# Adding expert results up by token in DRAM instead of collecting one row per choice

## The chip, the cores and the metric

The kernel runs on one core of a Trainium2 chip. The core has a matrix engine (PE, with its weight loads shown as PEld), a vector engine (DVE), an activation engine (ACT), a general engine (POOL), which also issues the indirect DMAs, and a sequencer (SP), which issues most of the others. All DMAs share 16 DMA engines. Each engine works through its own instructions in the order in which they stand, and waits for the others by semaphores. The metric is the device time of one execution in microseconds. The matrix engine's clock is granted by a throttle; the profile shows the share.

## The reference, cut to what matters

Two layers run over 8 sequences of 256 tokens, 2048 tokens of 256 features in fp32. Each sublayer is followed by a layernorm over token plus result.

```python
x = L0_attn_x
x = _layernorm(x + _L0_attn_ref(x, ...))   # 16 heads, causal
x = _layernorm(x + _L0_ffn_ref(x, ...))    # 32 experts, 6 of them for each token
x = _layernorm(x + _L1_attn_ref(x, ...))   # a state-space mixer
x = _layernorm(x + _L1_ffn_ref(x, ...))    # 16 experts, 4 of them for each token
...
# a mixture: what is added to a token is the weighted sum of its experts, and a shared expert
act = jax.nn.silu(g) * u
routed = jnp.einsum('tef,efd,te->td', act, wd, combine)
shared = jax.nn.silu(hidden_states @ sg) * (hidden_states @ su) @ sd
return routed + shared
```

The change is about `routed`: `combine` is nonzero for 6 (or 4) experts of a token, and the sum over `e` has to bring together results that are computed in different places.

## The kernel before

Tokens are worked on in 16 tiles of 128 (`P`), in 4 groups (`NG`) of 4 tiles (`GT`). The tokens' rows stay on the chip all the time, as `xg[g][:, t, :]`.

**Stages.** The attention of the first layer runs group by group, up to about 700 us. Beside it, `route` works out, for each group, which experts a token takes, and POOL scatters a copy of the token's row to each of its experts' bucket in DRAM (`xs`, line 381). A row has 256 features and two words more: the number of the place where its result belongs (`dest`, from an iota), and its weight. Buckets are blanked at the start (`blank_buckets`, line 218): unfilled rows then carry the number `NOWHERE`. That is 105 MB of writes on SP's queue, beside the first 300 us of attention.

Then the first mixture M0 (`mixture`, `Experts.routed`). The filled rows are cut into 112 tiles of 128 rows of one expert. `step` is a software pipeline over tiles: SP loads the tile's rows (`xl`, line 653), 8 tiles ahead; PE turns them and DVE copies them out (`xT`, line 520); PE multiplies with the expert's gate and up weights (`gu`), ACT and DVE make the hidden rows (`s`, `h`), PE turns them (`hp`), DVE copies them (`hT`), PE multiplies with the down weights (`y`, line 573), ACT scales by the weight into `ys` (line 680, three buffers), and POOL scatters the 128 result rows to DRAM (line 681). The place is the number in the row: token times 6 plus the choice, so each of the 2048 x 6 results has a row of its own, and a row of `NOWHERE` is dropped by the bounds check. Since no two scatters touch the same row, `unordered` tells the scheduler that they need not wait for each other. They wait on POOL only for their `ys`.

After the last tile, `results` (line 706) has SP load, for each token tile, its 128 x 6 rows (768 KB, one DMA); it waits for all scatters. `summed` (line 775; groups 0 and 1) adds the upper half of the 6 to the lower half on DVE (128x768), has PE add the remaining 3 by matmuls with the identity, and adds that to the token; `combined` (line 765; groups 2 and 3) does all of it on DVE. `normed` is the layernorm. This is woven into the mixer of the second layer, which begins with group 0 as soon as its tokens are normed.

The second mixture M1 works in the same way: 72 tiles, its rows scattered beside the mixer, 2048 x 4 results. Its end (`after1`, line 1596) is the kernel's end: 16 gathers of 512 KB go into the large weight buffer `big`, beside the shared expert of the last group; then `finish` for each token tile: `summed`, `normed`, and the output DMA from ACT.

**What sets the order.** A scheduler orders each engine's instructions by their dependences; waits are put in by it for each reader and writer of a tile, of a buffer of a pool and of a DRAM array. `rowpool` has four buffers with the tag `r`, which `blank`, the scatters' sources `xe` and the gathered `gy` take in turn.

Of the kernel before, what the change touches and what calls it, by code (L numbers as in the profile page):

```python
# [38 lines left out]
class Moe:  # L39
# [6 lines left out]

    def __init__(self, name, n, f, top, halves, sh, ahead):
        self.name, self.n, self.f, self.top = name, n, f, top  # L50
        self.ahead = ahead
        self.tiles = (NTOK * top - n) // P + n
        self.rows = n * NTOK + (self.tiles - NTOK * top // P) * P

        self.sure = -(-((NG - 1) * GN * top - n * (P - 1)) // P)
        self.halves, self.fh = halves, f // halves


        self.usual = NTOK * top // P + n // 2

        self.cols = KC * 2 * f + halves * DM
        self.shwidth, self.shblocks = feature_blocks(sh)
        self.shcols = KC * self.shwidth + len(self.shblocks) * DM
# [20 lines left out]

NOWHERE = 1 << 20
ROW = DM + 2
M0 = Moe("m0", E0, F0, TOP0, 1, SH0, 8)
M1 = Moe("m1", E1, F1, TOP1, 2, SH1, 5)

ED = 512  # L90
HS, PD, ND = 8, 64, 64
# [8 lines left out]
def kernel(  # L100
# [84 lines left out]
    )  # L185


    disp = {}
    for m in (M0, M1):
        d = disp[m.name] = {}  # L190
        new = lambda shape, name, dt=F32: const.tile(
            shape, dt, name=f"{m.name}{name}", tag=f"{m.name}{name}"
        )
        d["xs"] = dram.tile([m.rows, ROW], F32, name=f"{m.name}xs", tag=f"{m.name}xs")

        d["ys"] = dram.tile([NTOK * m.top, DM], F32, name=f"{m.name}ys", tag=f"{m.name}ys")
# [12 lines left out]
        nc.gpsimd.iota(  # L209
            d["dest"], pattern=[[P * m.top, NTOK // P], [1, m.top]], base=0,  # L210
            channel_multiplier=m.top,
        )
        run = small.tile([P, m.n], F32, name=f"{m.name}run", tag=f"{m.name}run", bufs=2)
        nc.vector.memset(run, 0.0)
        d["run"] = run
        d["scatters"], d["results"], d["loads"], d["first"] = [], [], [], None
# [290 lines left out]
    class Experts:  # L507
# [114 lines left out]
        def routed(self, w, beside=None):  # L622
# [21 lines left out]
            def step(s, lo, hi):  # L644
# [31 lines left out]
                if lo <= i < hi:  # L676
                    y = self.down(hT.pop(i), wdn, bass.ds(experts[i], 1), f"{m.name}{i}")
                    row = xl.pop(i)
                    ys = self.sb.tile([P, DM], F32, name=f"{m.name}ys{i}", tag="ys", bufs=3)
                    nc.scalar.activation(ys, y, AF.Copy, scale=row[:, DM + 1 :])  # L680
                    ins = nc.gpsimd.indirect_dma_start(  # L681
                        out=d["ys"],
                        out_offset=bass.IndirectOffsetOnAxis(
                            ap=row[:, DM : DM + 1].bitcast(I32), axis=0
                        ),
                        in_=ys, in_offset=None, bounds_check=NTOK * m.top - 1, oob_is_err=False,
                    )
                    unordered(ins, f"{m.name}ys", d["results"])
                extra()
                if beside and s >= 4 and s % 2 == 0:  # L690
                    next(beside, None)
# [14 lines left out]
    def results(m, g, t, gy=None):  # L706

        d, i = disp[m.name], g * GT + t
        if gy is None:
            gy = rowpool.tile([P, m.top, DM], F32, name=f"{m.name}gy{g}_{t}", tag="r")  # L710
        ins = nc.sync.dma_start(
            gy,
            d["ys"][i * P * m.top : (i + 1) * P * m.top, :].rearrange(
                "(p k) d -> p k d", k=m.top
            ),
        )
        d["first"] = after_all(ins, d["first"], d["results"])
        return gy

    def root_by_steps(y, v):  # L720

# [42 lines left out]

    def combined(m, g, t, gy):

        half = m.top // 2
        x = xg[g][:, t, :]
        nc.vector.tensor_add(gy[:, :half, :], gy[:, :half, :], gy[:, half:, :])
        nc.vector.tensor_add(x, x, gy[:, 0, :])  # L770
        for k in range(1, half):
            nc.vector.tensor_add(x, x, gy[:, k, :])
        normed(g, t)

    def summed(m, g, t, gy, y=None, behind=None):

        half = m.top // 2
        x = xg[g][:, t, :]
        ins = nc.vector.tensor_add(gy[:, :half, :], gy[:, :half, :], gy[:, half:, :])  # L779
        if behind is not None:  # L780
            tc.add_manual_dep(ins.ins, behind.ins.name, NOSYNC, reason="it waits for longer")
# [7 lines left out]
        nc.vector.tensor_add(x, x, y)  # L789
        normed(g, t)  # L790

    def top_weights(scores, n_exp, top):
# [114 lines left out]
    with ExitStack() as st:  # L907
# [30 lines left out]
        nc.gpsimd.memset(blank[:, :, DM : DM + 1].bitcast(I32), NOWHERE)  # L938
        blank_buckets(M0, blank)
        blank_buckets(M1, blank)  # L940

        def project_v(g, q, xT):
            vs = []
# [652 lines left out]
    def after1(ex):  # L1596

        last = (NG - 1) * GT
        order = [0, 1, last, 2, 3, last + 1, 4, 5, 6, 7, last + 2, 8, 9, last + 3, 10, 11]

        rows = {}
        for n, i in enumerate(order):
            gy = big[:, n * TOP1 * DM : (n + 1) * TOP1 * DM]
            rows[i] = results(M1, *divmod(i, GT), gy.rearrange("p (k d) -> p k d", d=DM))

        def finish(i, y=None):
            g, t = divmod(i, GT)
            summed(M1, g, t, rows.pop(i), y)
            nc.scalar.dma_start(out_rows[i * P : (i + 1) * P, :], xg[g][:, t, :])

        steps = ex.shared(NG - 1, wsh1, lambda t, y: finish(last + t, y))
        for _ in range(len(M1.shblocks)):
            next(steps)
        for i in order:
            if i >= last:
                if i == last + 2:
                    next(steps)
                next(steps)
            else:
                finish(i)  # L1620
# [96 lines left out]
```

## Time and profile before

| | us |
|---|---|
| median of 17 runs | 1509.02 (1499.89 to 1514.05) |
| the profiled execution | 1500.77 |
| its span, first to last instruction | 1499.1 |
| PE busy | 1410.1 (94%) |
| DVE busy | 820.1 (55%) |
| ACT busy | 545.7 (36%) |
| POOL busy | 461.8 (31%) |
| result scatters on POOL, M0 | 112 of 989 ns |
| result scatters on POOL, M1 | 72 of 984 ns |

The profile is one execution; its busy times are the time that an engine had work under way. The page cuts the span into 40 slices of 37.5 us: the DMA engines are busy nine tenths in the first eight (the blanks), hardly at all up to about 560 us, then loaded with the expert weights and the mixtures' rows; the granted clock falls below full in the slices around 710, 950 and 1250 us, where PE has pauses. HBM is read for 79.77 MB and written for 154.88 MB.

### The profile page before, as it was taken

To read this page: it belongs to the slowest core of one execution; us is meant where nothing else is said; L and a number is where in the kernel's file an instruction comes from. 1 tells how busy PE (TensorE), PEld (TensorE's weight loads), DVE (VectorE), ACT (ScalarE), POOL (GpSimd) and SP (SyncE) were. 2 spreads that over 40 slices of the span, in tenths; PEclk is the share of its full clock that TensorE was granted. 3 is DMA by queue.
4 is the path that set the end of the run, shared out by engine and by line. 5 is a ranking of instruction groups with operands and counts; after the bars stand their busy time and mean duration, and the time that the engine had idled before them with its cause. 6 is when DMAs were issued, how large, how long until landed. Compare 5 with 4: busy or idle time off the path is not lost. (4 is left out here: it accounts for less than half of the span.)

```text
span 1499.1 us, 21445 instructions
## 1 busy us (share of the span) xinstructions
PE 1410.1 (94%) x6424; PEld 1006.7 (67%) x6424; DVE 820.1 (55%) x3004; ACT 545.7 (36%) x1453; POOL 461.8 (31%) x684
## 2 busy tenths in 40 slices
PE   8999999999999999997788898889999989999997
PEld 4666666676666666666667776546577767777766
DVE  3444465555544465545345554488678864544436
ACT  3333342333333333333234433255655432233323
POOL 1000003500052000621655556102006275633335
PEclk9999999999999999998899999799999989999999
DMA  9999999930010001242345443530001542333327
GB/s 361 413 413 413 413 411 400 364 73 1 7 50 30 0 1 60 106 157 90 121 123 187 130 145 116 222 118 32 1 1 58 210 142 89 107 107 96 96 90 265
DMA packets 79206, 232.97 MB, mean 155 GB/s; under 512 B 11067, under 2 KB 43610, under 8 KB 77680
## 3 DMA queue, kind: packets, MB, share of 16 engines
q1 hardware_dynamic: 60208, 187.26, 34.3%
q0 software_dynamic: 16576, 42.19, 7.9%
q10 hardware_dynamic: 2304, 2.10, 0.4%
q8 instruction: 56, 0.92, 0.2%
q14 instruction: 62, 0.51, 0.1%
HBM read 79.77 MB, written 154.88 MB: 157 GB/s over the span
## 5 line engine op out<-in xcount | busy, mean ns | idle before, releaser
L963 PE MATMUL qkp<-xT,big 128*128 128x512 f32 x512 | 241.2, 593 | 0.0
L998 ACT ACTIVATE pr<-neg,least 128x128 f32<-128x128 f32 (+1 forms) x256 | 114.3, 448 | 283.7 <-DVE least L993 276.1
L971 DVE COPY qk<-qkp 128x512 f32<-128x512 f32 x64 | 44.2, 690 | 176.8 <-PE qkp L963 176.7
L963 PEld LDWEIGHTS qkp<-xT,big 128*128 128x128 f32 x512 | 90.7, 191 | 69.4 <-issue 67.9
L681 POOL DMA_INDIRECT m0ys<-m0ys,m0xl x112 | 110.8, 989 | 84.8 <-issue 25.9
L381 POOL DMA_INDIRECT m0xs<-m0xe,m0rows x96 | 94.8, 988 | 111.5 <-DVE total L1002 33.9
L947 PE MATMUL vp<-big,xT 128*128 128x512 f32 x256 | 118.4, 601 | 4.6 <-DVE x L1034 4.6
L1029 PE MATMUL op<-big,z 128*128 128x256 f32 x512 | 120.5, 382 | 0.0
L993 DVE CUSTOM_DVE_ANT_0 neg<-sc,cmask 128x128 f32<-128x128 f32 (+1 forms) x256 | 81.3, 355 | 59.9 <-PE sc L983 58.8
L1029 PEld LDWEIGHTS op<-big,z 128*128 128x128 f32 x512 | 92.6, 190 | 15.0 <-ACT z L1051 4.2
L681 POOL DMA_INDIRECT m1ys<-m1ys,m1xl x72 | 70.8, 984 | 98.8 <-ACT m1ys L680 90.6
L260 POOL TENSOR_TENSOR rstd<-rstd,numbers 128x1 f32<-128x1 f32 x16 | 8.7, 551 | 282.7 <-DVE rstd L259 282.7
L947 PEld LDWEIGHTS vp<-big,xT 128*128 128x128 f32 x256 | 47.2, 193 | 49.7 <-issue 42.4
L1016 PE MATMUL zp<-pT,big 128*128 128x256 f32 x256 | 76.8, 381 | 0.1
L983 PE MATMUL sc<-qk,qk 128*128 128x256 f32 x256 | 76.5, 380 | 0.0
L1004 DVE TENSOR_SCALAR pr<-pr,total 128x128 f32<-128x128 f32 (+1 forms) x256 | 73.4, 336 | 3.4
L381 POOL DMA_INDIRECT m1xs<-m1xe,m1rows x64 | 63.0, 985 | 20.1 <-POOL m1xe L376 12.5
L1010 PEld LDWEIGHTS pt<-ident,pr 128*128 128x128 f32 x384 | 47.4, 142 | 32.4 <-issue 29.8
L1014 DVE COPY pT<-pt 128x384 f32<-128x384 f32 x128 | 67.0, 549 | 2.9 <-PE pt L1010 2.1
L1016 PEld LDWEIGHTS zp<-pT,big 128*128 128x128 f32 x256 | 47.7, 190 | 30.4 <-issue 12.0
L979 PEld LDWEIGHTS sc<-qk,qk 128*128 128x128 f32 x256 | 43.7, 190 | 22.4 <-issue 20.2
L953 ACT COPY big<-vp 128x512 f32<-128x512 f32 x53 | 31.0, 585 | 74.8 <-PE vp L947 74.8
(2756 smaller groups left out, 3024.5 us busy)
## 6 DMA issues: line engine op xcount, KB each, us to landing
m0xs<-blank SPq DMA_DIRECT2D x9, 7740.0 KB
m1xs<-blank SPq DMA_DIRECT2D x4, 7740.0 KB
m0xl<-m0xs SPq DMA_DIRECT2D x112, 129.0 KB
m0gy<-m0ys SPq DMA_DIRECT2D x16, 768.0 KB
m1xl<-m1xs SPq DMA_DIRECT2D x72, 129.0 KB
big<-m1ys SPq DMA_DIRECT2D x16, 512.0 KB
big<-in_w_moe SPq DMA_DIRECT2D x1, 5472.0 KB
big<-in_w_heads SPq DMA_DIRECT2D x12, 384.0 KB
```

Source lines behind the costliest of these rows:

```text
L381: ins = nc.gpsimd.indirect_dma_start(out=d["xs"], out_offset=bass.IndirectOffsetOnAxis(ap=rows[:, k, t : t + 1], axis=0), in_=xe[:, k, :], ...
L681: ins = nc.gpsimd.indirect_dma_start(out=d["ys"], out_offset=bass.IndirectOffsetOnAxis(ap=row[:, DM : DM + 1].bitcast(I32), axis=0), in_=y ...
L947: nc.tensor.matmul(ps, lhsT=xT[:, k, t * P : (t + 1) * P], rhs=w_vq[q][:, k, :], start=(k == 0), stop=(k == KC - 1),)
L963: nc.tensor.matmul(ps, lhsT=w_qk[h][:, at : at + P], rhs=xT[:, k, :], start=(k == 0), stop=(k == KC - 1),)
L983: nc.tensor.matmul(sc[:, P:], lhsT=qT[:, c0 + P : c0 + SEQ], rhs=kT[:, c0 : c0 + SEQ], start=True, stop=True,)
L993: nc.vector.tensor_tensor_reduce(out=neg[:, cols], in0=sc[:, cols], in1=cmask[:, cols], scale=-SCALE, scalar=3.0e38, op0=ALU.add, op1=ALU.min,
L998: nc.scalar.activation(pr[:, cols], neg[:, cols], AF.Exp, bias=least[:, i : i + 1], scale=-1.0, accum_out=total[:, i : i + 1],)
L1004: nc.vector.tensor_scalar_mul(pr[:, cols], pr[:, cols], total[:, i : i + 1])
L1010: nc.tensor.transpose(pt[:, i * P : (i + 1) * P], pr[:, i * P : (i + 1) * P], ident)
L1014: pace[0] = nc.vector.tensor_copy(pT, pt)
L1016: nc.tensor.matmul(zps[:, b * SEQ : (b + 1) * SEQ], lhsT=vs[2 * b][:, cols], rhs=pT[:, : 2 * P], start=True, stop=False,)
L1029: nc.tensor.matmul(ps[:, :DM], lhsT=zs[i][:, t * P : (t + 1) * P], rhs=w_o[q * QH + i], start=(i == 0), stop=(i == QH - 1),)
```

## The change

Each result row is no longer stored in a place of its own, but added in DRAM to a row that belongs to its token. M0 has three such arrays, M1 two (`sums`); tile i adds to array i modulo `sums`. So the scatter gets `compute_op=ALU.add`, `dest` holds the token's number alone, and the arrays have 2048 + 128 rows. Since additions to one array must not overlap, `unordered` is gone: each scatter waits for the landing of the one before it in the same array. The bounds check is gone too: a DVE instruction takes the smaller of the row's number and `nobody`, which is 2048 plus the partition, so that unfilled rows are added to 128 rows that nobody reads. The arrays must begin at zero: a tile of zeros is written over all five at the start, 15 DMAs on SP behind the blanks.

Gathering takes `sums` DMAs of 128 KB a token tile for M0 (3 x 16 in place of 16), and 2 DMAs of 256 KB for each pair of token tiles for M1 (16 in place of 16, of half the size). `summed` and `combined` have no pairwise addition any more.

```diff
@@ Moe, its two instances
-M0 = Moe("m0", E0, F0, TOP0, 1, SH0, 8)
-M1 = Moe("m1", E1, F1, TOP1, 2, SH1, 5)
+M0 = Moe("m0", E0, F0, TOP0, 1, SH0, 8, 3)
+M1 = Moe("m1", E1, F1, TOP1, 2, SH1, 5, 2)
@@ at the start
+    nobody = const.tile([P, 1], I32, name="nobody", tag="nobody")
+    nc.gpsimd.iota(nobody, pattern=[[0, 1]], base=NTOK, channel_multiplier=1)
...
+            d["ys"] = [
+                dram.tile([NTOK + P, DM], F32, name=f"{m.name}ys{i}", tag=f"{m.name}ys{i}")
+                for i in range(m.sums)
+            ]
...
-            d["dest"], pattern=[[P * m.top, NTOK // P], [1, m.top]], base=0,
-            channel_multiplier=m.top,
+            d["dest"],
+            pattern=[[P, NTOK // P], [0, m.top]] if m.sums
+            else [[P * m.top, NTOK // P], [1, m.top]],
+            base=0, channel_multiplier=1 if m.sums else m.top,
@@ step, the scatter of a tile's results
-                    ins = nc.gpsimd.indirect_dma_start(
-                        out=d["ys"],
-                        out_offset=bass.IndirectOffsetOnAxis(
-                            ap=row[:, DM : DM + 1].bitcast(I32), axis=0
-                        ),
-                        in_=ys, in_offset=None, bounds_check=NTOK * m.top - 1, oob_is_err=False,
-                    )
-                    unordered(ins, f"{m.name}ys", d["results"])
+                    if m.sums:
+                        to = self.sb.tile([P, 1], I32, name=f"{m.name}to{i}", tag="to", bufs=4)
+                        nc.vector.tensor_tensor(
+                            to, row[:, DM : DM + 1].bitcast(I32), nobody, ALU.min
+                        )
+                        d["results"].append(nc.gpsimd.indirect_dma_start(
+                            out=d["ys"][i % m.sums],
+                            out_offset=bass.IndirectOffsetOnAxis(ap=to, axis=0),
+                            in_=ys, in_offset=None, compute_op=ALU.add,
+                        ))
...
@@ results
+    def sums_of(m, gy, g, t, n):
+
+        at = (g * GT + t) * P
+        for i, ys in enumerate(disp[m.name]["ys"]):
+            nc.sync.dma_start(
+                gy[:, :, i, :], ys[at : at + n * P, :].rearrange("(t p) d -> p t d", p=P)
+            )
@@ combined and summed
-        half = m.top // 2
+        half = m.sums or m.top // 2
...
-        nc.vector.tensor_add(gy[:, :half, :], gy[:, :half, :], gy[:, half:, :])
+        if not m.sums:
+            nc.vector.tensor_add(gy[:, :half, :], gy[:, :half, :], gy[:, half:, :])
@@ behind the blanks
+        zeros = rowpool.tile([P, 6, DM], F32, name="zeros", tag="r")
+        nc.gpsimd.memset(zeros, 0.0)
+        for m in (M0, M1):
+            for ys in disp[m.name]["ys"] if m.sums else ():
+                n = (NTOK + P) // P
+                for at in range(0, n, 6):
+                    c = min(6, n - at)
+                    nc.sync.dma_start(
+                        ys[at * P : (at + c) * P, :].rearrange("(p c) d -> p c d", p=P),
+                        zeros[:, :c, :],
+                    )
@@ after1, the kernel's end
-        for n, i in enumerate(order):
-            gy = big[:, n * TOP1 * DM : (n + 1) * TOP1 * DM]
-            rows[i] = results(M1, *divmod(i, GT), gy.rearrange("p (k d) -> p k d", d=DM))
+        pairs = [0, last, 2, 4, 6, last + 2, 8, 10]
+        for n, i in enumerate(pairs):
+            gy = big[:, n * 2 * M1.sums * DM : (n + 1) * 2 * M1.sums * DM].rearrange(
+                "p (t k d) -> p t k d", t=2, d=DM
+            )
+            sums_of(M1, gy, *divmod(i, GT), 2)
+            rows[i], rows[i + 1] = gy[:, 0], gy[:, 1]
```

More of the change, by code (lines that the diff above doesn't have):

```diff
@@ L39, with __init__ @@
 class Moe:
-    def __init__(self, name, n, f, top, halves, sh, ahead):
+    def __init__(self, name, n, f, top, halves, sh, ahead, sums):
         self.name, self.n, self.f, self.top = name, n, f, top
         self.ahead = ahead
+        self.sums = sums
         self.tiles = (NTOK * top - n) // P + n
@@ L194 @@
         d["xs"] = dram.tile([m.rows, ROW], F32, name=f"{m.name}xs", tag=f"{m.name}xs")
-        d["ys"] = dram.tile([NTOK * m.top, DM], F32, name=f"{m.name}ys", tag=f"{m.name}ys")
+        if m.sums:
[3 more added lines that the diff above has]
+            ]
+        else:
+            d["ys"] = dram.tile(
+                [NTOK * m.top, DM], F32, name=f"{m.name}ys", tag=f"{m.name}ys"
+            )
         d["base"] = new([P, m.n], "base")
@@ L680, in step @@
                     nc.scalar.activation(ys, y, AF.Copy, scale=row[:, DM + 1 :])
-                    ins = nc.gpsimd.indirect_dma_start(
-                        out=d["ys"],
-                        out_offset=bass.IndirectOffsetOnAxis(
-                            ap=row[:, DM : DM + 1].bitcast(I32), axis=0
-                        ),
-                        in_=ys, in_offset=None, bounds_check=NTOK * m.top - 1, oob_is_err=False,
-                    )
-                    unordered(ins, f"{m.name}ys", d["results"])
+                    if m.sums:
+                        to = self.sb.tile([P, 1], I32, name=f"{m.name}to{i}", tag="to", bufs=4)
[7 more added lines that the diff above has]
+                        ))
+                    else:
+                        ins = nc.gpsimd.indirect_dma_start(
+                            out=d["ys"],
+                            out_offset=bass.IndirectOffsetOnAxis(
+                                ap=row[:, DM : DM + 1].bitcast(I32), axis=0
+                            ),
+                            in_=ys, in_offset=None, bounds_check=NTOK * m.top - 1, oob_is_err=False,
+                        )
+                        unordered(ins, f"{m.name}ys", d["results"])
                 extra()
@@ L709, in results @@
         if gy is None:
-            gy = rowpool.tile([P, m.top, DM], F32, name=f"{m.name}gy{g}_{t}", tag="r")
+            gy = rowpool.tile([P, m.sums or m.top, DM], F32, name=f"{m.name}gy{g}_{t}", tag="r")
+        if m.sums:
+            sums_of(m, gy.unsqueeze(1), g, t, 1)
+            return gy
         ins = nc.sync.dma_start(
@@ L775, in summed @@
     def summed(m, g, t, gy, y=None, behind=None):
-        half = m.top // 2
+        half = m.sums or m.top // 2
         x = xg[g][:, t, :]
-        ins = nc.vector.tensor_add(gy[:, :half, :], gy[:, :half, :], gy[:, half:, :])
-        if behind is not None:
-            tc.add_manual_dep(ins.ins, behind.ins.name, NOSYNC, reason="it waits for longer")
+        if not m.sums:
+            ins = nc.vector.tensor_add(gy[:, :half, :], gy[:, :half, :], gy[:, half:, :])
+            if behind is not None:
+                tc.add_manual_dep(ins.ins, behind.ins.name, NOSYNC, reason="it waits for longer")
         fresh = y is None
@@ L788, in summed @@
             )
-        nc.vector.tensor_add(x, x, y)
+        ins = nc.vector.tensor_add(x, x, y)
+        if m.sums and behind is not None:
+            tc.add_manual_dep(ins.ins, behind.ins.name, NOSYNC, reason="it waits for longer")
         normed(g, t)
@@ L940 @@
         blank_buckets(M1, blank)
+        zeros = rowpool.tile([P, 6, DM], F32, name="zeros", tag="r")
[8 more added lines that the diff above has]
+                        zeros[:, :c, :],
+                    )
         def project_v(g, q, xT):
@@ L1601, in after1 @@
         rows = {}
-        for n, i in enumerate(order):
-            gy = big[:, n * TOP1 * DM : (n + 1) * TOP1 * DM]
-            rows[i] = results(M1, *divmod(i, GT), gy.rearrange("p (k d) -> p k d", d=DM))
+        pairs = [0, last, 2, 4, 6, last + 2, 8, 10]
+        for n, i in enumerate(pairs):
+            gy = big[:, n * 2 * M1.sums * DM : (n + 1) * 2 * M1.sums * DM].rearrange(
+                "p (t k d) -> p t k d", t=2, d=DM
+            )
+            sums_of(M1, gy, *divmod(i, GT), 2)
+            rows[i], rows[i + 1] = gy[:, 0], gy[:, 1]
         def finish(i, y=None):
```

## The prediction

> **What bounds the kernel now.** I read the table by stage first, because the page's share of 94% for PE is a mean over unlike stages.
>
> ```profile
> core 0: us, PE busy (x) PEld busy (x) DVE busy (x) ACT busy (x) POOL busy (x), PEclk, DMA share, GB/s
> 790.00:936.00 146.00, 127.36 (x754) 107.75 (x753) 72.20 (x257) 58.07 (x170) 85.88 (x87) 1.00 0.45 140
> 960.00:1000.00 40.00, 34.53 (x98) 19.83 (x98) 26.00 (x65) 19.42 (x33) 2.77 (x8) 0.79 0.32 115
> 1000.00:1200.00 200.00, 191.32 (x984) 135.59 (x984) 161.13 (x566) 111.64 (x246) 48.18 (x90) 0.98 0.17 67
> 1300.00:1470.00 170.00, 166.28 (x788) 124.58 (x788) 73.61 (x208) 51.46 (x129) 66.43 (x71) 0.98 0.35 113
> 1470.00:1499.00 29.00, 19.39 (x87) 15.44 (x85) 19.31 (x69) 9.54 (x17) 16.34 (x43) 0.94 0.63 227
> ```
>
> 790 to 936 us is the first mixture's steady part: PE is busy 127 of 146 us, so some other engine's lateness is in the pace. 1300 to 1470 is the second mixture: PE 98%, nothing to gain or to lose until something else gets slower than PE. The two places where sums are collected (960 to 1000, 1470 to 1499) have PE gaps. Then POOL's own timeline, which shows the pace of the result scatters (columns: start, duration, and in brackets the idle time before and what ended it):
>
> ```profile
> 837.03 0.98 POOL L681 DMA_INDIRECT m0ys<-m0ys,m0xl  x1 [0.30 <-issue]
> 838.32 0.98 POOL L681 DMA_INDIRECT m0ys<-m0ys,m0xl  x1 [0.30 <-issue]
> 840.78 0.98 POOL L681 DMA_INDIRECT m0ys<-m0ys,m0xl  x1 [1.48 <-ACT m058s L533]
> 1360.24 0.98 POOL L681 DMA_INDIRECT m1ys<-m1ys,m1xl  x1 [1.51 <-ACT m1ys L680]
> 1362.72 0.98 POOL L681 DMA_INDIRECT m1ys<-m1ys,m1xl  x1 [1.51 <-ACT m1ys L680]
> 1456.34 0.98 POOL L681 DMA_INDIRECT m1ys<-m1ys,m1xl  x1 [1.82 <-ACT m1ys L680]
> ```
>
> In the first mixture POOL goes as fast as it can (0.98 + 0.30 = 1.29 us), then rests: tile 24 issues at 790.00 and tile 111 at 936.16, so 146.16 / 87 = 1.68 us a tile. In the second it is even, 2.49 us a tile, with 1.51 us to spare. Last, what a scatter takes to land, read where somebody waits for it:
>
> ```profile
> 1452.17 0.47 ACT L680 ACTIVATE m1ys<-m170y,m1xl 128x256 f32<-128x256 f32 x1 [0.57 <-DMA m1ys<-m1ys,m1xl]
> 1455.59 0.47 ACT L680 ACTIVATE m1ys<-m171y,m1xl 128x256 f32<-128x256 f32 x1 [2.95 <-DMA m1ys<-m1ys,m1xl]
> 1458.98 20.79 SPq L711 DMA_DIRECT2D big<-m1ys  x16
> 1462.23 0.69 DVE L779 TENSOR_TENSOR big<-big 128x512 f32<-128x512 f32 x1 [1.04 <-DMA big<-m1ys]
> ```
>
> The last scatter issues at 1456.34 and SP, which waits for it, starts the gathers at 1458.98: 2.64 us from issue to landing. The first gather needs 1462.23 - 1458.98 = 3.25 us until DVE has its rows. The two ACT rows show the end of the mixture waiting for scatters three tiles back (three `ys` buffers).
>
> **Fill.** 5 arrays of 2176 rows of 1 KB are 11.1 MB more on SP's queue behind the blank rows, which go at 413 GB/s by the page's slices: 27 us. No scatter of the first mixture's rows waits for them, since they are issued last. But the `zeros` tile holds one of four row buffers, and POOL's copy into that buffer waits for the fill. These are the rows where the like wait ends now, and POOL's next work:
>
> ```profile
> 306.42 0.23 POOL L369 COPY m0xe<-m0dest 128x6 int32<-128x6 int32 x1 [7.76 <-DMA m0xs<-m0xe,m0rows]
> 340.99 1.09 POOL L260 TENSOR_TENSOR rstd<-rstd,numbers 128x1 f32<-128x1 f32 x2 [34.34 <-DVE rstd L259]
> ```
>
> 306.4 + 27 = 333.4, and POOL is wanted at 341.0 for group 1's layernorm: hidden, with 7.6 us of cover; without it each us late delays that layernorm. The memset (the blank's, of the same size, is 1.43 us) lies in POOL's idle first 170 us. Zero.
>
> **Index.** 184 `min` operations of 128x1 on DVE at 0.15 us (DVE's 128x1 TENSOR_TENSOR). DVE is half idle in both mixtures (72 of 146, 74 of 170 us). In the changed program's order the `min` of tile k stands before the xT copy of tile k+4 and waits for the landing of scatter k-4 (four `to` buffers); behind it are that copy, hT and h, so a late landing reaches PE two steps on. In exchange a row load no longer waits for the scatter that read its index: that wait wasn't binding. Zero by itself; its wait is part of the loop below.
>
> **The new waits.** A scatter now waits on POOL for the one three tiles back (first mixture) or two back (second), because it adds to the same array. What stands behind it on POOL is the next scatter, and early in the mixture row scatters. The first of these is no news: ACT already waits for the scatter three back, through its buffer. So both are one loop: landing, ACT 0.47 us, hand to POOL 0.28, a hop of 0.1, next landing. Three tiles cost at least L + 0.85 us, and 3 x 1.68 = 5.04, so the pace holds while L, the time from issue to landing, is under 4.2 us. In the second mixture the loop is L + about 0.15 for two tiles against 4.98: L may be 4.8.
>
> No row shows an adding scatter. From below: as a plain one, 2.64. From above: the plain one and a whole gather (a read of DRAM) in series, 2.64 + 3.25 = 5.9. I take the middle, 4.3, since 128 rows must be read as well as written but the read needn't be a whole 512 KB gather. POOL's 0.98 us per scatter is bounded likewise: 0.98, or twice that if the reads' descriptors cost as much as the writes'; nearest is 0.98 with some more, which the 1.68 covers up to 1.4.
> At L = 4.3 the loop gives (4.3 + 0.85) / 3 = 1.72 us: 0.04 x 87 = 3 us. Besides, PE's work is 127.4 / 87 = 1.46 us a tile, and the other 0.22 comes from releases that arrive late. Once the loop has no slack, such a delay is partly on top: between 0 and 0.22 x 87 = 19 us; I take half, 9. Together +12. The second mixture: (4.3 + 0.15) / 2 = 2.2 < 2.49, zero. At the end of each mixture PE waits for a buffer, that is for a landing (the 2.95 us above): 1.6 us later each, +3.
>
> The Trainium skill (DMA: Bandwidth & Descriptors, Anatomy of one DMA) fits a POOL-issued DMA as 2.0 us plus its bytes at 436 GB/s; for 128 KB that is 2.3 us, where the row has 2.64. Doubling the bytes there, an estimate, adds only 0.3 us, and by it no loop binds and the sum is the gains alone. The same page (Rules for kernel authors) says that an accumulate reads its destination and writes it later, so that the earlier DMA's semaphore must be waited for: the waits can't be dropped. No run here shows that.
>
> **Gains.** The reads halve (768 to 384 KB, 512 to 256 KB a token tile) and the first pairwise add goes.
>
> ```profile
> L769 DVE TENSOR_TENSOR m0gy<-m0gy 128x768 f32<-128x768 f32 x8 | 7.6, 950 | 3.6 <-DMA m0gy<-m0ys 3.6
> L779 DVE TENSOR_TENSOR m0gy<-m0gy 128x768 f32<-128x768 f32 x8 | 7.6, 955 | 1.7 <-DMA m0gy<-m0ys 1.7
> L779 DVE TENSOR_TENSOR big<-big 128x512 f32<-128x512 f32 x16 | 10.8, 677 | 1.9 <-DMA big<-m1ys 1.9
> ```
>
> That is 26 us of DVE, but PE's work stays as it was (the matmul count by `summed` is 3 and 2 as before), so only PE's gaps can close: 1.3 us before the first sum at 949.2 (its gather is hidden beside the shared expert, 935 to 948, and so is the time that SP needs for three DMAs in place of one); 2.3 us of PE at 976 to 978 where DVE is full; 0.4 in 1000 to 1200, at 96%; and in the tail the PE gaps of 0.2, 0.5 and 1.3 us between 1481 and 1486, plus 1 us of POOL's queue of norms. Sum -7.
>
> **Sum.** +12 + 3 - 7 = +8 us on the profiled execution's own 1500.77 us (span 1499.1): 1509. That execution is 8.25 us under the median 1509.02; on the median's scale 1517.
>
> **Rivals.** Nothing binds (L under 4.2, POOL under 1.4): the gains less a little at the ends, -7 + 1: 1503, faster. For it: the plain landing has 1.5 us of slack, and 16 DMA engines are busy only 0.45. Against: the first mixture already issues in bursts. It decides at L = 4.2.
> Cancelled: gains and losses within 3 us of each other, 1509.
> Adding is dear: L = 5.9 gives 6.75 / 3 = 2.25 us, +0.57 x 87 = 50, and the second mixture 3.0 against 2.49 over 58 tiles (1305 to 1450 us), +31; ends +6, gains -7: 1589. Or POOL at 2 x 0.98 + 0.30 = 2.27 a tile: +51, 1556. Against it: the packets' share of the engines is small.
> That PE's gaps are not closed at all, since other waits stand behind them, takes the -7 away: 1524, within the forecast.
>
> **How the numbers follow.** Forecast 0.37 (own range 1512 to 1530), nothing binds 0.35, cancelled 0.12, dear 0.16. About 0.2%, 3 us, is what a measurement can tell from no change: faster 0.35, same 0.12, slower 0.53. The range runs from a little under 1503 to where about half of the dear case is cut off: 1500 to 1562.
>
> **What would show it.** The scatters' spacing between 790 and 936 (1.68 now; I say about 1.8), and the second mixture's 2.49 unchanged; POOL idle before a scatter put down to the scatter itself rather than to ACT; PE's restart after each mixture; the copy after the fill near 333. If the fill ends after 341, if DMA_INDIRECT takes over 1.4 us, or if the second mixture's pace moves, I'm wrong.

## The result, and the profile after

The changed kernel takes 1546.65 us (median, 1544.31 to 1551.93), the kernel before 1508.64 beside it: ratio 1.0261, 95% interval 1.0244 to 1.0278. That is 38 us more, where 8 were forecast. The profiled execution takes 1543.65 us, span 1541.9, which is 42.8 more than the first profile of before (1499.1).

The kernel before itself has two times: 1507 to 1509 beside the result and e1 to e8, 1471 to 1473 beside e9 to e18, at a granted clock of 0.972 and 0.978; one chip appears on both sides. Its traces tell the two apart (e13). Every ratio below is with runs of the kernel before taken beside it. Where times from the two sides are compared with each other, the time of before is given.

Where the 42.8 us lie, read from the POOL, DVE and PE timelines of the two profiles:

| | before | after | later by |
|---|---|---|---|
| result scatter of tile 24, first mixture | 790.0 | 799.4 | 9.4 |
| last result scatter of the first mixture (tile 111) | 936.2 | 971.2 | 35.0 |
| last matmul of the mixer's output (`out`) ends | 1232.3 | 1254.9 | 22.6 |
| DVE starts the last group's routing (`mx`) | 1244.1 | 1278.9 | 34.9 |
| first result scatter of the second mixture | 1281.3 | 1316.6 | 35.3 |
| last one | 1456.3 | 1499.2 | 42.8 |
| end of the span | 1499.1 | 1541.9 | 42.8 |

So there are three losses (first mixture 35, start of the second 12, inside the second 8) and a gain of 12 between the mixtures. The two mixtures' steady parts by the table by stage, with the columns that the prediction showed:

```profile
core 0: us, PE busy (x) PEld busy (x) DVE busy (x) ACT busy (x) POOL busy (x), PEclk, DMA share, GB/s
799.00:970.00 171.00, 135.56 (x756) 110.16 (x755) 74.06 (x338) 62.13 (x170) 134.56 (x88) 0.98 0.78 126
1340.00:1512.00 172.00, 165.82 (x777) 123.28 (x776) 70.07 (x253) 50.96 (x127) 101.24 (x70) 0.98 0.64 108
```

In the first, 87 tiles take 171.7 us (1.97 each) where they took 146.2; POOL is as busy as PE, and the DMA engines' share is 0.78 where it was 0.45, though fewer bytes move a second. DVE is no busier. The page's costliest groups after, where each line ends with the busy time, the mean of one, and the idle time before them with what ended most of it:

```profile
L703 POOL DMA_INDIRECT m0ys<-m0ys,m0to x112 | 174.6, 1559 | 55.8 <-issue 12.8
L703 POOL DMA_INDIRECT m1ys<-m1ys,m1to x72 | 112.0, 1555 | 65.6 <-ACT m1ys L697 10.3
L700 DVE TENSOR_TENSOR m0to<-m0xl,nobody 128x1 int32<-128x1 int32 x112 | 18.0, 160 | 124.9 <-DMA m0ys<-m0ys,m0to 118.7
L700 DVE TENSOR_TENSOR m1to<-m1xl,nobody 128x1 int32<-128x1 int32 x72 | 11.5, 160 | 109.1 <-DMA m1ys<-m1ys,m1to 92.5
```

Two things are new. An adding scatter holds POOL for 1.56 us where the plain one took 0.99. And DVE stands idle 125 + 109 us in front of the 184 index minima, nine tenths of it (118.7 + 92.5) waiting for a scatter's landing: 118.7 / 112 = 1.06 us for each of the first mixture's. The minima themselves are 0.16 us. How much of this idle time reaches the kernel's time, the experiments show. POOL's timeline, which showed bursts and rests before, has scatters as close as they go, and some rests put down to a landing:

```profile
855.39 1.55 POOL L703 DMA_INDIRECT m0ys<-m0ys,m0to  x1 [0.44 <-DMA m0ys<-m0ys,m0to]
857.25 1.56 POOL L703 DMA_INDIRECT m0ys<-m0ys,m0to  x1 [0.30 <-DMA m0ys<-m0ys,m0to]
859.11 1.55 POOL L703 DMA_INDIRECT m0ys<-m0ys,m0to  x1 [0.30 <-ACT m059s L550]
```

DVE's timeline in the first mixture's steady part (start, duration, in brackets the idle time before and what ended it):

```profile
857.14 0.16 DVE L700 TENSOR_TENSOR m0to<-m0xl,nobody 128x1 int32<-128x1 int32 x1 [0.91 <-DMA m0ys<-m0ys,m0to]
857.22 0.42 DVE L537 COPY m059xT<-m059xp 128x256 f32<-128x256 f32 x1
857.57 0.28 DVE L563 COPY m056hT<-m056hp 96x128 f32<-96x128 f32 x1
857.76 0.24 DVE L552 TENSOR_TENSOR m058h<-m058s,m058gu 128x96 f32<-128x96 f32 x1
859.58 0.16 DVE L700 TENSOR_TENSOR m0to<-m0xl,nobody 128x1 int32<-128x1 int32 x1 [1.58 <-DMA m0ys<-m0ys,m0to]
```

The copy xT, the copy hT and the product h run without a pause once the minimum is through: they were ready and stood behind it. Between the mixer and the second mixture, the same view shows the 12 us. First the last group's routing in the kernel before, then the changed kernel:

```profile
1244.06 0.22 DVE L832 TENSOR_REDUCE mx<-m1lg 128x4 f32<-128x64 f32 x1 [3.02 <-issue]
```

```profile
1263.37 0.42 DVE L580 TENSOR_TENSOR m1s_1h<-m1s_1s,m1s_1gu 128x256 f32<-128x256 f32 x1 [1.03 <-ACT m1s_1s L579]
1276.73 0.16 DVE L700 TENSOR_TENSOR m1to<-m1xl,nobody 128x1 int32<-128x1 int32 x1 [12.94 <-DMA m1xl<-m1xs]
...
1278.87 0.16 DVE L700 TENSOR_TENSOR m1to<-m1xl,nobody 128x1 int32<-128x1 int32 x1 [0.33 <-DMA m1xl<-m1xs]
1278.94 0.22 DVE L875 TENSOR_REDUCE mx<-m1lg 128x4 f32<-128x64 f32 x1
```

The logits `m1lg` were ready at 1266.8 (the end of their matmuls), but four minima of the second mixture's first tiles stand ahead of `mx` in DVE's order, and they wait for row loads. SP issues these at 1274.59, 3 us after POOL has issued the last scatter of the rows that they read:

```profile
1264.92 1.85 PE L325 MATMUL m1lg<-w_gate,m1xT 128*128 128x16 f32 x16
1271.61 0.98 POOL L398 DMA_INDIRECT m1xs<-m1xe,m1rows  x1 [0.28 <-POOL m1xe L393]
1274.59 5.52 SPq L670 DMA_DIRECT2D m1xl<-m1xs  x10
```

Nobody waited that early before, because the first user of a row was PE; there `mx` starts 0.04 us behind the end of the logits.

At the kernel's end the last scatter issues at 1499.16 and SP's gathers, which wait for its landing, follow 2.94 us later (2.64 before):

```profile
1499.16 1.55 POOL L703 DMA_INDIRECT m1ys<-m1ys,m1to  x1 [0.70 <-DMA m1ys<-m1ys,m1to]
1502.10 11.16 SPq L755 DMA_DIRECT2D big<-m1ys  x16
```

### The profile page after: what moved, and what is told of

It reads as the page before. It is cut to its first block, busy times and chain, and to the rows that moved or that the text cites. A ratio compares the mean times of both kernels' runs of the same rounds, so it can differ in the third digit from the quotient of the medians.

```text
span 1541.9 us, 21653 instructions
## 1 busy us (share of the span) xinstructions
PE 1421.7 (92%) x6424; PEld 1010.0 (65%) x6424; DVE 804.7 (52%) x3156; ACT 550.7 (36%) x1453; POOL 562.8 (37%) x686
## 3 DMA queue, kind: packets, MB, share of 16 engines
q0 software_dynamic: 34240, 45.32, 17.1%
## 4 chain that ended last, share of the span: by engine, by line
PE 68%; DMA 12%; issue 8%; POOL 6%; DVE 4%; ACT 1%; POOLq 0%; DVEq 0%; ACTq 0%; SPq 0%
PE qkp L1017 14%; DMA m0ys<-m0ys,m0to 7%; PE vp L1001 7%; PE op L1083 6%; PE zp L1070 4%; PE sc L1037 4%; DMA m1ys<-m1ys,m1to 3%; PE pt L1064 3%; POOL m1xs L398 3%; PE sc L1033 2%; PE cv L1268 2%; PE zp L1074 2%; PE gtp L1443 2%; DMA m1xs<-m1xe,m1rows 1%; PE sg L1381 1%
## 5 line engine op out<-in xcount | busy, mean ns | idle before, releaser
L703 POOL DMA_INDIRECT m0ys<-m0ys,m0to x112 | 174.6, 1559 | 55.8 <-issue 12.8
L703 POOL DMA_INDIRECT m1ys<-m1ys,m1to x72 | 112.0, 1555 | 65.6 <-ACT m1ys L697 10.3
L700 DVE TENSOR_TENSOR m0to<-m0xl,nobody 128x1 int32<-128x1 int32 x112 | 18.0, 160 | 124.9 <-DMA m0ys<-m0ys,m0to 118.7
L700 DVE TENSOR_TENSOR m1to<-m1xl,nobody 128x1 int32<-128x1 int32 x72 | 11.5, 160 | 109.1 <-DMA m1ys<-m1ys,m1to 92.5
```

Source lines behind the costliest of these rows:

```text
L703: d["results"].append(nc.gpsimd.indirect_dma_start(out=d["ys"][i % m.sums], out_offset=bass.IndirectOffsetOnAxis(ap=to, axis=0), in_=ys, i ...
```

## The experiments

**e1: the minima late.** The scheduler is told to put a tile's minimum behind the newest `hT` copy on DVE.

```diff
-            nc.vector.tensor_copy(hT, ps)
+            self.turn = nc.vector.tensor_copy(hT, ps)
...
-                        nc.vector.tensor_tensor(
+                        ins = nc.vector.tensor_tensor(
                             to, row[:, DM : DM + 1].bitcast(I32), nobody, ALU.min
                         )
+                        tc.add_manual_dep(ins.ins, self.turn.ins.name, NOSYNC, reason="late")
```

> The changed kernel with one order added: the index minimum of a tile stands on DVE behind the newest hT copy, so that it can't run ahead of the routing of the last group. Nothing is left out. In the changed kernel DVE stood 12.9 us before the first four minima of the second mixture (1263.8 to 1276.7 us), whose rows weren't there yet, and the routing behind them was late by that. Theory A (these early minima cost the whole stall): the mixture starts 12 us earlier, 1546.65 - 12 = about 1535. Theory B (the stall only covers another wait of the routing): no more than 3 us less, 1544 or more. For the first mixture: if its 1.97 us a tile is POOL's 1.55 + 0.30 with DVE's waits for landings (the minima's) on top, its 87 tiles come down to 1.86 x 87 = 162 us from 172, 10 us more, and the time is 1525; if the landings themselves bind, the pace stays at 1.97.

1514.91 us beside 1507.01: 1.0051 (1.0032 to 1.0070). 32 of the 38 us are gone with one line of order and nothing else changed. Theory A holds, and more came than the 1525 to 1535 expected. The groups and DVE's timeline of e1:

```profile
L700 DVE TENSOR_TENSOR m0to<-m0xl,nobody 128x1 int32<-128x1 int32 x112 | 17.3, 154 | 7.7 <-DMA m0ys<-m0ys,m0to 7.5 <-issue 0.2
L700 DVE TENSOR_TENSOR m1to<-m1xl,nobody 128x1 int32<-128x1 int32 x72 | 11.1, 155 | 3.3 <-DMA m1ys<-m1ys,m1to 2.5 <-DVE m1to L700 0.8
```

```profile
1254.28 0.23 DVE L876 TENSOR_REDUCE mx<-m1lg 128x4 f32<-128x64 f32 x1 [3.02 <-PE m1lg L325]
```

The idle time before the minima is 11 us in place of 234, and the routing starts on the logits. The first mixture's pace comes to 1.911 us a tile, not to POOL's 1.86.

**e6: late in the first mixture alone** (e1's dependency under `if m is M0`).

> The changed kernel with late minima in the first mixture alone; those of the second stay early. Nothing is left out. It splits the 32 us between the two mixtures. If the second mixture's share is the routing stall (12 us) and its pace (2.54 in place of 2.45, 5 us): 1515 + 17 = about 1530, between 1526 and 1534. If the first mixture's pace is most of it: under 1522.

1535.53 beside 1508.02. So the early minima cost 1546.65 - 1535.53 = 11 us in the first mixture and 1535.53 - 1514.91 = 21 in the second, over the 17 expected (1535.53 is just outside the 1526 to 1534). `mx` is 13.5 us behind the logits there, and tiles 8 to 66 of the second mixture take 2.57 us each, in e1 2.45.

**e12: eight index buffers in place of four** (`bufs=8`; `xl` has one buffer less).

> The changed kernel with eight index buffers in place of four (one row buffer less for want of room). Nothing is left out. A reader's first remedy for a wait on four buffers. In the program's order the minimum of tile k then stands as much earlier as its buffer comes free earlier, so it still waits for the newest landing. Theory (the place in the order is the cost): no help, the pace of the first mixture stays above 1.95 and eight minima stand before the second mixture's routing in place of four: 1544 or more. Rival (four buffers are too few): the pace falls to 1.91 and the time by 10 us or more, to 1536 or less.

1562.36 us (two runs), against 1546.65 (before at 1508) and 1552.84 (e14, before at 1472) with four: no help. In DVE's order the minimum of tile k now stands ahead of the xT copy of tile k, where with four buffers it stood ahead of that of tile k+4: the longer queue is used to put the minima four tiles earlier. Five minima stand ahead of `mx`, not the eight expected; `mx` is 14.2 us behind the logits, the first mixture's pace 2.11 (2.10 in e14).

**e11: no minima.** `to` is the row's own number, and the adding scatter gets the bounds check back.

```diff
-                        nc.vector.tensor_tensor(
-                            to, row[:, DM : DM + 1].bitcast(I32), nobody, ALU.min
-                        )
+                        to = row[:, DM : DM + 1].bitcast(I32)
...
                             in_=ys, in_offset=None, compute_op=ALU.add,
+                            bounds_check=NTOK - 1, oob_is_err=False,
```

> The changed kernel without the index minima: the adding scatter keeps the bounds check that the kernel before had, and unfilled rows are dropped by it. Nothing is left out. No DVE instruction waits for a landing any more, and none stands ahead of the routing. Theory (the minima's place in DVE's order is the cost, not their 0.16 us of work): the same as e1 with its late minima, 1511 to 1518. Rival (the scatter's waits, which now come through the row buffers, or the check in the scatter cost): over 1520.

1516.67 us, within 2 us of late minima (e1's 1514.91, though before is at 1471 here and at 1507 there): the place is the cost, not the work. POOL's 1.56 us a scatter stays.

**e4 and e17: the new waits alone**, in the kernel before.

```diff
                     unordered(ins, f"{m.name}ys", d["results"])
+                    n = 3 if m is M0 else 2
+                    if len(d["results"]) > n:
+                        tc.add_manual_dep(
+                            ins.ins, d["results"][-1 - n].ins.name, SYNC, reason="one at a time"
+                        )
```

> The kernel before with the new waits alone: each result scatter waits for the one three back (first mixture) or two back (second), plain scatters of 0.98 us into rows of their own. Theory POOL: plain landings are early enough (2.64 us, under 4.2), the pace stays at 1.68, the time within 4 us of before: 1505 to 1513. Theory landing: the pace goes up by 0.1 us or more, +9 us or more: 1518 and above.

> e4 once more (the kernel before with the waits between scatters alone), which was the same as before at 1508. Where the kernel before runs at 1473: 1471 to 1477 if a landing takes under 3.6 us when scatters are 1.47 us apart; 1485 or more if the waits bring the pace up to 1.6 or more.

0.9999 (0.9978 to 1.0020) beside 1507.01, 0.9998 (0.9985 to 1.0010) beside 1472.45. With plain landings the waits are free at either pace. What they cost with the longer landing of an adding scatter, these two can't tell; e8 and e10 bear on that.

**e3 and e16: POOL's time alone**, in the kernel before: one more small POOL instruction behind each result scatter, 0.58 us.

```diff
...
+                    more = nc.gpsimd.tensor_tensor(spare, ones[:, :1], root[:, :1], ALU.pow)
+                    tc.add_manual_dep(more.ins, ins.ins.name, NOSYNC, reason="behind it")
...
```

> The kernel before with one 128x1 power on POOL (0.55 us) after each result scatter, and nothing else of the change: POOL then needs 0.98 + 0.55 and the gaps, about 1.8 to 1.95 us a tile, like the adding scatter's 1.86, with no new waits, no minima and no more DMA work. Theory POOL: the first mixture's pace goes from 1.68 to 1.9 - 2.0, +19 to +28 us, and the first tiles, where row scatters alternate with results, add some 5: 1530 to 1542. Theory landing: POOL's issue has slack, and the time stays under 1514.

> e3 once more (the kernel before with 0.57 us more of POOL per scatter). POOL needs 1.81 us a tile whatever the releases do, so against 1.47 it should now cost (1.81 - 1.47) x 87 = 30 us in the first mixture where it cost 4.8 against 1.68: 1500 to 1512 beside 1473. Rival (POOL's price is hidden as it was): 1480 or less.

e3: 1511.80 beside 1507.01, 1.0039 (1.0020 to 1.0058): 5 us, far under the 23 to 35 that the theory asked for, though the pace went to 1.825. e16: 1514.45 beside 1472.45, 1.0280 (1.0260 to 1.0300): 42 us, more than the 30. The kernel with the burden takes nearly the same time in both; it is the kernel without it that differs.

**e13: the kernel before, with a trace from where it takes 1473.**

> The kernel before, unchanged, with a profile of its own. In the last call its runs took 1471.5 us beside 1508 in all earlier ones, at the same granted clock (0.978), and e9 to e12 were compared with those. Reading A (something outside the kernel's own order, in that call alone): 1505 to 1510 again, and the profile's stages lie within some 6 us of the first one's: first mixture at 1.68 us a tile, second at 2.49. Reading B (the kernel before has a second speed of its own): it comes up in some of these runs as well, near 1471, and if the profiled run is one of them its stages show where 36 us are saved, the second mixture's 2.49 us a tile first.

1473.93 beside 1473.04: reading B, but the second mixture is not where the time is saved. Its POOL timeline, in place of the bursts and rests that the prediction showed:

```profile
839.73 0.98 POOL L681 DMA_INDIRECT m0ys<-m0ys,m0xl  x1 [0.43 <-ACT m0ys L680]
841.14 0.98 POOL L681 DMA_INDIRECT m0ys<-m0ys,m0xl  x1 [0.43 <-ACT m0ys L680]
842.56 0.98 POOL L681 DMA_INDIRECT m0ys<-m0ys,m0xl  x1 [0.43 <-ACT m0ys L680]
843.97 0.98 POOL L681 DMA_INDIRECT m0ys<-m0ys,m0xl  x1 [0.43 <-ACT m0ys L680]
```

It is even, 1.41 us apart here and 1.471 from tile 24 to 111, where the first profile had 1.680: (1.680 - 1.471) x 87 = 18 us, and tile 24 is 11 us earlier: the 29 us between the two spans. The second mixture is 2.494 in both. What differs is how soon ACT follows PE. These are the `gu` matmuls of a tile and ACT's silu of them, first in the first profile (0.65 us from the one's end to the other's start), then in e13 (0.04):

```profile
842.15 0.81 PE L528 MATMUL m060gu<-big,m060xT 128*128 x4
843.61 0.25 ACT L533 ACTIVATE m060s<-m060gu 128x96 f32<-128x96 f32 x1 [1.01 <-PE m056y L573]
```

```profile
839.00 0.81 PE L528 MATMUL m070gu<-big,m070xT 128*128 x4
839.85 0.25 ACT L533 ACTIVATE m070s<-m070gu 128x96 f32<-128x96 f32 x1 [0.40 <-PE m070gu L528]
```

In the first profile the silu starts over 0.6 us after the end of the matmuls in 31 of the first mixture's last 86 tiles (in 21 of them ACT stood idle just before), here in 2. The other traces with plain scatters in the first mixture and nothing added on POOL fall apart in the same way: e2, e4, e5 and e7, beside a before of 1507 or 1508, have 16 to 31 such tiles, e15, e17 and e18, beside 1472 or 1473, have 2 to 5. Each engine has its instructions of the first mixture in the same order in both traces of before, so it isn't another schedule. What makes the releases late was not found.

**e14: the changed kernel where before takes 1472.**

> The changed kernel, unchanged, beside a kernel before that now runs at 1473 us because its first mixture goes at PE's own 1.47 us a tile (e13) where it went at 1.68 with late releases. Theory (the changed kernel's first mixture is set by POOL's 1.86 and DVE's waits, whatever the releases do): 1540 to 1550 as before, +70 us over the kernel before. Rival (its 1.97 held late releases too): 1510 to 1525. If the kernel before comes at 1508 here, +38 as measured.

1552.84 beside 1472.45: 1.0544 (1.0527 to 1.0562), 80 us. It is 6 us slower than in the result, a little over the 1540 to 1550 expected, where the kernel before is 36 us faster. There was nothing for it to gain: the silu is over 0.6 us late in 1 of its 86 tiles here, and in 1 of 86 in its first profile as well.

**e2, e5 and e15: no addition.** The changed kernel with `compute_op=ALU.add` left out (e2), and the same with late minima (e5, e15).

> The changed kernel with plain scatters in place of adding ones: what is left out is the addition in DRAM, so each array holds the last result written to a token and the output is not the reference's. Waits between scatters, index minima, fill and halved gathers stay. Theory POOL (the adding scatter costs POOL 1.55 us in place of 0.98, and 1.86 us a tile sets the first mixture's pace): the scatter goes back to 0.98 us, tile 24 to 111 takes 1.68 to 1.75 us a tile in place of 1.97, and the time falls by 20 to 25 us in the first mixture and some 5 among the first tiles of both: 1515 to 1522. Theory landing (the wait for the scatter before in the same array sets it): the pace stays between 1.9 and 1.97 and the time above 1538.

> e1 with plain scatters: late minima, waits between scatters, fill and halved gathers, and no addition in DRAM (left out, so the output is not the reference's). What remains is waits, which cost nothing by e4, and the gains. Theory: the gains are there (half the gather, no pairwise sums, -4 to -7 us): 1500 to 1503 against before's 1507, and e1 minus this, some 12 to 15 us, is what the adding itself costs. Rival: the gains never reach PE, and it is the same as before, 1506 to 1509; then adding costs 6 to 9 us. With the early minima of e2 gone, the routing stall of 12 us before the second mixture must be gone too.

> e5 once more (plain scatters, late minima, halved gathers; the addition is left out), which was 6.7 us under the kernel before at 1508. Where the kernel before runs at 1473: if waits, minima and gathers cost or gain the same there, 1464 to 1470; if the waits for landings bind at 1.47 us a tile (three tiles are 4.4 us, less 0.85 leaves 3.6 us for a landing), its first mixture stays at 1.6 to 1.7 and it takes 1485 to 1502.

e2: 1514.88 beside 1507.01, 1.0043 (1.0017 to 1.0069). Pace 1.726, and the routing stall is still there (`mx` 14.4 us behind the logits). e5: 1501.28 beside 1508.02, 0.9960 (0.9940 to 0.9980): a gain of 6.7. e15: 1460.19 beside 1472.45, 0.9918 (0.9900 to 0.9937): a gain of 12.3, more than expected. Waits, late minima, fill and gathers together are better than free. The rest of the change's price is the addition: 1514.91 - 1501.28 = 14 us by e1 and e5, 1516.67 - 1460.19 = 56 by e11 and e15 (before at 1471 and 1472; e11 has no minima at all, e15 late ones).

The two causes don't simply add up. Late minima alone take off 32 us (e1), and so does leaving out the addition alone (e2); both together take off 45 (e5). So the early minima cost 1514.88 - 1501.28 = 14 us with plain scatters and 32 with adding ones.

**e8 and e10: freer landings in the first mixture.** e1 with `M0 = Moe("m0", E0, F0, TOP0, 1, SH0, 6, 6)`, five `ys` and eight `to` buffers (e8); e9 with four arrays, four `ys` buffers and `ahead` 7 (e10).

> e1 with six arrays, five ys buffers and eight index buffers in the first mixture (row loads six tiles ahead for want of room): no scatter waits for a landing soon after it. Nothing is left out, but the gathers have six rows again and three more arrays are filled. Theory POOL: the pace of tiles 24 to 111 goes from 1.91 to POOL's own 1.86 and not under it. Theory landing: it falls towards 1.68. The fill of 8 arrays, 17.8 MB at 413 GB/s, takes 43 us from 306, to 349: the layernorm of group 1 on POOL (at 341 now) should be some 8 us late, and the whole kernel that much later if nothing makes up for it.

> e9 with four arrays and four ys buffers (row loads seven tiles ahead for want of room): a scatter waits for the one four back. Nothing is left out; a token has four rows to gather in place of three. Theory POOL: the pace is 1.86 to 1.87 as in e8 with six arrays, since POOL's own 1.55 + 0.30 is left, and the time is 2 to 5 us under e9's: 1506 to 1510, no better than before. Theory landing: e8's six were needed, and it stays near 1.91.

e8's POOL has no idle time left but the 0.30 us after each scatter:

```profile
856.79 1.55 POOL L704 DMA_INDIRECT m0ys<-m0ys,m0to  x1 [0.30 <-DVE m070xT L537]
858.65 1.55 POOL L704 DMA_INDIRECT m0ys<-m0ys,m0to  x1 [0.30 <-DVE m071xT L537]
860.51 1.55 POOL L704 DMA_INDIRECT m0ys<-m0ys,m0to  x1 [0.30 <-ACT m070s L550]
```

From tile 24 to 111 it is 1.861 us a tile: POOL's floor, so POOL is the bound. In e1 ACT waits 8 times, up to 2.9 us, for the landing that frees its `ys` buffer, and POOL's longer pauses follow such waits; all of the looser waits together are worth the other 0.05 of e1's 1.911, 4 us, at most. Counted from tile 26 it is 1.890 in e1, 0.03 more than e8. As a whole e8 takes 1526.12 (two runs) beside 1508.02: from the first mixture's last scatter to the end of the mixer's output it needs 304 us, e1 285, and there six rows a token are gathered again. Its longer fill was expected to make the layernorm of group 1 late by 8 us; that starts at 341.32, as before:

```profile
341.32 1.09 POOL L277 TENSOR_TENSOR rstd<-rstd,numbers 128x1 f32<-128x1 f32 x2 [32.46 <-DVE rstd L276]
```

e10: 1516.14 where 1506 to 1510 was expected, pace 1.901. The time is a miss, but the pace isn't against theory POOL: 1.901 holds two pauses before tiles 25 and 26, of 3.1 and 1.0 us, while the granted clock is 0.57 (787 to 796 us) and PE is busy all the time; from tile 26 to 111 it is 1.861, as in e8. So four arrays and four `ys` buffers are enough. The time is lost between the mixtures, where the fourth row is gathered: 293 us from the last scatter to the mixer's end, in e9 285.

**e7 and e9: one mixture alone.** e1 with `sums` 0 for the first mixture (e7), or for the second (e9), which then runs as before.

> The first mixture as before (plain scatters, six rows a token gathered), the second as in e1 (adds in two arrays, late minima). Nothing is left out. If POOL's 1.55 us costs only where POOL sets the pace (1.86 against 1.68 in the first mixture, against 2.49 in the second): within 4 us of before, 1504 to 1511. If adding costs by itself (landings, DMA work) in the second too: 1512 or more, and the pace of the second mixture's tiles 8 to 66 is above 2.5.

> The first mixture as in e1 (adds in three arrays, late minima), the second as before (plain scatters, four rows a token gathered). Nothing is left out. If the two mixtures' costs add up, this is e1's +7.9 less e7's +3 to +4: 4 us above before, 1510 to 1513, with a first mixture of 1.91 us a tile. If adding in the first mixture is all of the cost and e7's part something else: 1515 or more.

e7: 1512.45 beside 1508.02, 1.0019 (1.0003 to 1.0036), a little over the 1504 to 1511 expected. Tiles 8 to 66 go at 2.451, no slower than the 2.494 of before, so 1.86 us under 2.49 is hidden; what is lost is at the ends: the eight first scatters, which alternate with row scatters, take 23.8 us in place of 21.4, and the last five intervals 11.1 in place of 9.0, with ACT waiting for landings as the prediction said. e9: 1511.27, as expected, but beside a kernel before at 1471.49: 1.0273 (1.0256 to 1.0290).

**e18: half the gather without adding.** The kernel before, with the first mixture's results stored as bf16 and added up in fp32. It rounds where the reference doesn't.

```diff
-        d["ys"] = dram.tile([NTOK * m.top, DM], F32, ...
+        d["ys"] = dram.tile([NTOK * m.top, DM], BF16 if m is M0 else F32, ...
...
-        nc.vector.tensor_add(gy[:, :half, :], gy[:, :half, :], gy[:, half:, :])
+        nc.vector.tensor_add(gy[:, :half, :], *halves_of(m, gy))
```

> The kernel before with the first mixture's results stored and gathered as bf16 (the second's as before, fp32), added up on DVE in fp32: the gathers are halved as in the changed kernel, without the addition in DRAM, minima, waits or fill; the pairwise sum on DVE stays. It rounds each of a token's six results to 8 bits, which the reference doesn't. If the gain of e5 and e15 (6.7 and 12.3 us) is the halved gather: 1460 to 1467 beside 1473, or 1501 to 1504 beside 1508. If it is the pairwise sum that is gone there, or the row loads that no longer wait: the same as before within 3 us.

1467.71 beside 1472.91: 0.9962 (0.9947 to 0.9978). Of e15's 12 us this keeps 5, between the two outcomes that were expected, and it is faster than both kernels. By the traces little of the 5 is the halved gather: at the first mixture's last scatter, before any gather, e18 is already 1.6 us ahead of e13 (904.99 against 906.58; its scatters carry half the bytes), and at the end of the mixer's output 3.2 (1201.82 against 1205.06). Between these two points it gains 1.7 us, and e15 11.8 (907.04 to 1193.74). So most of e15's gain is the pairwise sum that is gone or the row loads that no longer wait, which wasn't taken apart.

## Why the prediction was wrong, by its own steps

**Fill: zero.** Right: POOL's layernorm of group 1 starts at 341.15 (340.99 before):

```profile
341.15 1.09 POOL L277 TENSOR_TENSOR rstd<-rstd,numbers 128x1 f32<-128x1 f32 x2 [34.62 <-DVE rstd L276]
```

The copy that I had put ahead of it isn't the one that waits, as e8's longer fill shows, so there was more cover than 7.6 us. The fill ends near 340, not 333 (the DMA engines move 404 to 414 GB/s until then), and in e8 near 358.

**Index: "Zero by itself; its wait is part of the loop below."** This is the step that failed, and it is 32 of the 38 us (e1), 14 of which would be there with plain scatters too (e2 and e5). I had its place right, ahead of the xT copy of tile k+4 and behind the landing of scatter k-4, and priced it as if a landing under 4.2 us made that place harmless. But each time the landing comes later than DVE reaches the minimum, xT, hT and h of other tiles wait with it (118.7 us of DVE idle time in the first mixture, of which 11 us reach the kernel's time, e6). And I never asked what the first four minima of each mixture stand ahead of: in the second it is the routing of the last group, 12 us in the result and 13.5 in e6. The half idle DVE that I gave as cover doesn't cover a wait, only work.

**The new waits.** With plain landings they cost nothing (e4 and e17 are at 1.000), which the sum would have said too. With adding scatters they are worth at most the 4 us between e1 and e8, about the 3 us forecast, but on top of POOL's 1.86 a tile and not of 1.68. The 9 us of late releases on top are not there: the changed kernel has late releases in 1 of 86 tiles. A landing took 3.9 us in the median (below; 3.8 to 4.4 in the traces of e9 to e12 and e14, by mixture), near the 4.3 that I took. The profile's DMA lists of e14 and of e13 (last column: median us from issue to landing):

```profile
m0ys<-m0ys,m0to POOLq DMA_INDIRECT x112, 3.9
```

```profile
m0ys<-m0ys,m0xl POOLq DMA_INDIRECT x112, 2.7
```

The Trainium skill (DMA: Bandwidth & Descriptors, Anatomy of one DMA) gives an estimate of 2.6 us for the adding one, by its fit with the bytes counted twice; the measurement is 1.3 above that, and decides.

**POOL's price.** Bounded by 0.98 and 1.96, taken as "0.98 with some more" and covered to 1.4; it is 1.56, and so 1.86 a tile. That was one of my own signs of being wrong. Of the two ends I went to the nearer one without a reason. The sum has nothing for it; a POOL instruction of that size costs 5 us where releases are late and 42 where they are on time (e3, e16). The queue table of the profile shows what grows with it: the software queue has 34240 packets after and 16576 before, (34240 - 16576) / 184 = 96 more for each scatter: an adding one has 128 packets of 1 KB in the trace, where the plain one's are mostly of 4 KB. That the packets are what POOL's time goes into is likely and not shown.

**The first mixture's +12.** e1's last result scatter is at 957.4 and e5's at 945.6: 12 us, for another reason than mine (POOL's 1.86 in place of landings at 1.72). So the whole of e1, +7.9, agrees with the forecast of +8 by luck, not by its working: POOL costs most of what the waits and the late releases should have. Luck too is the rival of 1556, the number nearest to the result: it has POOL at 2.27 us a tile.

**Cover.** The 1.68 us a tile was taken as the kernel's own. I had seen that 0.22 of it were late releases, and still counted them as room for POOL and for landings. Where releases come on time the pace to compare with is 1.47, and the same POOL price is 42 us in place of 5 (e16, e3).

**Ends: +3.** For the second mixture's end I took 1.6 us; e7 has 2.1 there, for the reason given. Its 2.4 us at the start, where scatters alternate on POOL, I had not seen. **Gains: -7.** The sum is right, -6.7 (e5), and 12.3 where the first mixture is faster (e15). The places are not: I put 4 us between the mixtures and 3 in the tail, and by the traces of e13 and e15 it is 12 and 1.3.

**The second mixture unchanged.** Right for POOL (e7: 2.451), wrong with early minima: 2.54 in the changed kernel, 2.49 before. This was another of my signs.

## What to carry to other kernels

An instruction of 0.16 us on a half idle engine isn't free when it waits: ask for each new wait what stands behind it in that engine's order, in the first tiles as well as in the steady state, and where the scheduler's place for it holds up other work, give it one by hand (e1). More buffers moved the wait ahead and made it no better (e12). And before an idle share is spent as cover, ask whether it belongs to the kernel: the cover here was 0.21 us a tile of late releases, and it wasn't there in other runs of the same program, nor in the changed kernel.

## What the runs showed of the hardware

An adding indirect scatter of 128 rows of 1 KB took POOL 1.56 us (1.55 to 1.61 in the changed kernel), a plain one with a bounds check 0.98 to 0.99 on average, one without 0.96 (e5). From issue to landing the medians are 3.8 to 4.4 us for adding ones (e9 to e12, e14) and 2.4 to 2.7 for plain ones (e13, e15, e16). With the bounds check (e11) the adding one still took 1.56.

One program had two times 36 us apart; the 29 us between its two profiles lie in the first mixture alone, with the second mixture's pace at 2.494 in both. The cause is open. A kernel with more POOL time in that stage had nearly one time, 1511.80 and 1514.45 (e3, e16). No run has adding scatters without a wait between them.
